# Gate logits taken from channel-major tokens, with mean and deviation applied to the logits

## The chip, the core and the metric

The kernel runs on one core of a Trainium2 chip. The metric is device time in microseconds (us) from the first to the last instruction; before the change its median over 3 runs is 7140.85 us (7115.87 to 7148.11). The engines are TensorE (PE in the profile; PEld is its weight load), VectorE (DVE), ScalarE (ACT), GpSimd (POOL) and SyncE (SP). POOL and SP here mostly issue transfers. Each engine works through its own queue in order; engines wait for one another through semaphores.

## The reference

The input x is 4 x 256 x 64 x 64 in fp32. One MetaFormer layer is computed:

```python
x = x + conv(_ln_c(x))          # three modulated deformable 3x3 convolutions, each with relu
t = tokens(x)                   # 4 x 4096 tokens of 256 channels
t = t + ffn(_ln_t(t))           # mixture of 8 experts, the best 2 of each token
x = from_tokens(t)
```

`_ln_t` normalises a token over its 256 channels: (t - m) / sqrt(v + 1e-5). In the feed-forward part, with z the normalised tokens:

```python
logits = z @ gate_w + gate_b            # 256 x 8
probs = softmax(logits)
top2_vals, top2_idx = top_k(probs, 2)
out = sum over the two experts e of  prob_e * (gelu(z @ W1[e] + b1[e]) @ W2[e] + b2[e])
```

## The kernel before, in words

A batch is cut into 8 blocks of 512 positions (`BLK`), a block into 4 tiles of 128 tokens (`TPB`). The twelve stages (`self.stages`) are pairs of convolution layer and batch; each goes through 8 blocks, and each block through 9 taps. For a tap, GpSimd gathers four corners for 128 positions at a time (L494), VectorE blends them in two steps (L500, L505), ScalarE scales the sample (L508), TensorE transposes it (L523), ScalarE copies it out of PSUM (L526), and TensorE multiplies it with the weights of the tap into `acc` (L546). This is the main line of the program.

All other work is hung beside it in small pieces. Generators are put on a side list by `aside(steps, gen)`, and after every tap `step(k)` takes a share of that list, so that it is empty at the end of the block (`step` divides what is left by the taps that are left). The list is first in, first out. The expert work, the routing and the final sums are in three further lists, taken by `pump` after every tap. A scheduler then orders the instructions of each engine; `self.after(self.last)` asks that an operation is not placed ahead of the newest sample operation.

`tokens` (from L578) is the generator that the change touches. It runs once for each block of the third convolution layer, so in stages 3, 6, 9 and 11 (counted from 0), 32 times in all. Before the change it has 9 pieces:

1. the load of x for the residual,
2. the residual sum, `r` (L590), channel-major: channels on the partitions,
3. eight transposes of `r` into `tok`, token-major (L599), two copies out of PSUM (L604), and the store of `tok`,
4. the first half of `normalise`: mean and variance (L59, L60), square root on ScalarE (L62),
5. the second half: reciprocal (L65) and the normalised tokens `z` (L67); the store of `z` to DRAM, from which the experts later gather,
6. and 7. for two tiles each: four transposes of `z` back to channel-major (L622), a copy to `zT` (L628), the gate products (L632: the stationary operand is `zT`, the moving one the 8 gate columns), a copy of the logits to `lg` (L639),
8. gate bias, maximum, difference, exponential (L646 to L654),
9. softmax, rank of each expert, the two weights (L658 to L679).

`normalise` is also used ahead of the first convolution, by `pre_block`, whose pieces run beside stages 0, 3 and 6. All PSUM tiles tagged `tp` (transposes, logits, and others) share a pool of 3 buffers, `ps`. The tiles `zT` share 2 buffers with the experts' own `zT`. Tiles in the pool `small`, among them the mean and variance `mv`, the reciprocal `rs`, the logits `lg` and the probabilities `pr`, have one buffer each.

An fp32 product stands in the trace as two matmul records, a transpose as one.

Of the kernel before, what the change touches and what calls it, by code (L numbers as in the profile page):

```python
# [8 lines left out]
F32 = mybir.dt.float32  # L9
I32 = mybir.dt.int32  # L10
AF = mybir.ActivationFunctionType
ALU = mybir.AluOpType
AX = mybir.AxisListType

P = 128
H = W = 64
C = 256
CC = C // P
K = 9
NL = 3  # L20
TPB = 4
# [10 lines left out]
E = 8  # L32
# [19 lines left out]

def normalise(nc, pool, src, dst, eps, nm):

    T = src.shape[1]
    mv = pool.tile([P, T, nc.vector.BN_AGGR_DIM], F32, tag="mv", name=f"mv_{nm}")
    for t in range(T):
        st = pool.tile([P, nc.vector.BN_STATS_DIM], F32, tag="st", name=f"st_{nm}_{t}")
        nc.vector.bn_stats(st, src[:, t, :])  # L59
        nc.vector.bn_aggr(mv[:, t, :], st)  # L60
    sd = pool.tile([P, T], F32, tag="sd", name=f"sd_{nm}")
    nc.scalar.activation(sd, mv[:, :, 1], AF.Sqrt, bias=eps)  # L62
    yield
    rs = pool.tile([P, T], F32, tag="rs", name=f"rs_{nm}")
    nc.vector.reciprocal(rs, sd)  # L65
    for t in range(T):
        nc.vector.tensor_scalar(  # L67
            dst[:, t, :], src[:, t, :], mv[:, t, 0:1], rs[:, t : t + 1], ALU.subtract, ALU.mult
        )
# [37 lines left out]
class Weave:  # L107
# [94 lines left out]
    def ffn_constants(self):  # L202
        nc, cst, ins = self.nc, self.cst, self.ins
        self.t_dram = [
            [
                self.dram.tile([P, TPB, C], F32, name=f"t_{b}_{n}", tag=f"t_{b}_{n}")
                for n in range(NB)
            ]
            for b in range(self.B)
        ]  # L210
        nf = max(g.NF for g in self.groups)
        for g in self.groups:
            g.zd = self.dram.tile([g.M * P, C], F32, name=f"z_{g.nm}", tag=f"z_{g.nm}")
        self.ys = [
            self.dram.tile([nf * FT, C], F32, name=f"ys_{i}", tag=f"ys_{i}") for i in range(3)
        ]
        self.gw = cst.tile([P, CC, E], F32, name="gw")
        nc.sync.dma_start(self.gw, ins["gate_w"].rearrange("(c p) e -> p c e", p=P))
        self.gb = cst.tile([P, E], F32, name="gb")
        nc.sync.dma_start(self.gb, ins["gate_b"])  # L220

        self.before = cst.tile([P, E, E], F32, name="before")
        nc.vector.memset(self.before, 0.0)
        for e in range(1, E):
            nc.vector.memset(self.before[:, e, 0:e], 1.0)
        self.ones = cst.tile([P, P], F32, name="ones")
        nc.vector.memset(self.ones, 1.0)

        self.upper = cst.tile([P, P], F32, name="upper")
        nc.gpsimd.affine_select(  # L230
            self.upper, self.ones, pattern=[[1, P]], base=0, channel_multiplier=-1,
            compare_op=ALU.is_gt, fill=0.0,
        )

        self.fresh = {}
        for M in {g.M for g in self.groups}:
            fresh = cst.tile([P, E, M], F32, name=f"fresh_{M}")
            nc.vector.memset(fresh, 1.0)
            nc.vector.memset(fresh[:, :, 0:1], 0.0)
            self.fresh[M] = fresh  # L240
        part_i = cst.tile([P, 1], I32, name="part_i")
        nc.gpsimd.iota(part_i, pattern=[[0, 1]], base=0, channel_multiplier=1)
        self.part = cst.tile([P, 1], F32, name="part")
        nc.vector.tensor_copy(self.part, part_i)

        row_i = self.big.tile([P, P], I32, tag="hv", name="row_i")
        nc.gpsimd.iota(row_i, pattern=[[1, P]], base=0, channel_multiplier=0)
        self.row_f = cst.tile([P, P], F32, name="row_f")
        nc.vector.tensor_copy(self.row_f, row_i)
        assert FU * nf <= P  # L250
        self.token = cst.tile([P, NB * TPB], F32, name="token")
        nc.vector.tensor_scalar(
            self.token, self.row_f[:, : NB * TPB], float(P), self.part, ALU.mult, ALU.add
        )


        self.w = None
# [274 lines left out]
    def finish(self):  # L532

        if self.pend is None:
            return
        nc = self.nc
        i, n, k, sT, wins = self.pend
        self.pend = None
        l, b = self.stages[i]
        nm = f"{i}_{n}"  # L540
        if k == 0:
            self.acc = self.ps1.tile([P, CC, BLK], F32, tag="acc", name=f"acc_{nm}")
        acc = self.acc
        for o in range(CC):
            for c in range(CC):
                nc.tensor.matmul(  # L546
                    acc[:, o, :],
                    lhsT=self.wk[k][:, c, o * P : (o + 1) * P],
                    rhs=sT[:, c, :],
                    start=(k == 0 and c == 0),  # L550
                    stop=(k == K - 1 and c == CC - 1),
                )
        if n == NB - 1 and i + 1 < len(self.stages):
            self.load_tap(self.stages[i + 1][0], k, i + 1)
        if k < K - 1:
            return
        bk = self.bk[l]
        if l < NL - 1:
            w = wins[n] = self.window(n, nm, False)
            dst = [w[:, o, 1 : RPB + 1, :] for o in range(CC)]  # L560
            src = [acc[:, o, :].rearrange("p (r w) -> p r w", w=W) for o in range(CC)]
        else:
            r = self.big.tile([P, CC, BLK], F32, tag="a", name=f"r_{nm}")
            dst = [r[:, o, :] for o in range(CC)]
            src = [acc[:, o, :] for o in range(CC)]

        for o in range(CC):
            nc.scalar.activation(dst[o], src[o], AF.Relu, bias=bk[:, o : o + 1], scale=0.5)
        if l < NL - 1:
            self.rows_done(l + 1, b, n, wins)  # L570
        else:
            self.aside(9, self.tokens(b, n, r))

# [2 lines left out]
    def tokens(self, b, n, r):  # L578

        nc = self.nc  # L580
        nm = f"tok_{b}_{n}"
# [11 lines left out]
        z = self.big.tile([P, TPB, C], F32, tag="b", name=f"z_{nm}")  # L593
        lg = self.small.tile([P, TPB, E], F32, tag="lg", name=f"lg_{nm}")
        for t0 in range(0, TPB, 2):
            tp = self.ps.tile([P, 2, C], F32, tag="tp", name=f"tp_{nm}_{t0}")
            for t in range(2):
                for o in range(CC):
                    nc.tensor.transpose(  # L599
                        tp[:, t, o * P : (o + 1) * P],  # L600
                        r[:, o, (t0 + t) * P : (t0 + t + 1) * P],
                        self.ident,
                    )
            nc.scalar.copy(tok[:, t0 : t0 + 2, :], tp)  # L604
        nc.sync.dma_start(self.t_dram[b][n], tok)
        yield
        rest = normalise(nc, self.small, tok, z, self.eps_t, nm)
        with self.after(self.last):
            next(rest)
        yield  # L610
        with self.after(self.last):
            next(rest, None)
# [1 line left out]
        nc.sync.dma_start(  # L614
            grp.zd[r0 : r0 + BLK, :].rearrange("(t p) c -> p t c", p=P), z
        )
        for t0 in range(0, TPB, 2):
            yield
            tp = self.ps.tile([P, CC, 2 * P], F32, tag="tp", name=f"ztp_{nm}_{t0}")
            for t in range(2):  # L620
                for c in range(CC):
                    nc.tensor.transpose(  # L622
                        tp[:, c, t * P : (t + 1) * P],
                        z[:, t0 + t, c * P : (c + 1) * P],
                        self.ident,
                    )
            zT = self.ffn.tile([P, CC, 2 * P], F32, tag="zT", name=f"zT_{nm}_{t0}")
            nc.scalar.copy(zT, tp)  # L628
            lp = self.ps.tile([P, 2, E], F32, tag="tp", name=f"lp_{nm}_{t0}")
            for t in range(2):  # L630
                for c in range(CC):
                    nc.tensor.matmul(  # L632
                        lp[:, t, :],
                        lhsT=zT[:, c, t * P : (t + 1) * P],
                        rhs=self.gw[:, c, :],
                        start=(c == 0),
                        stop=(c == CC - 1),
                    )
            nc.scalar.copy(lg[:, t0 : t0 + 2, :], lp)  # L639

        def small(tag, shape):
            return self.small.tile(list(shape), F32, tag=tag, name=f"{tag}_{nm}")

        yield
        with self.after(self.last):
            nc.vector.tensor_tensor(  # L646
                lg, lg, self.gb.unsqueeze(1).to_broadcast([P, TPB, E]), ALU.add
            )
        mx = small("mx", (P, TPB))
        nc.vector.tensor_reduce(mx, lg, AX.X, ALU.max)  # L650
        nc.vector.tensor_tensor(
# [8 lines left out]
        pr = small("pr", (P, TPB, E))  # L660
# [446 lines left out]
```

## Time and profile before

| | |
|---|---|
| time, median of 3 | 7140.85 us |
| span of the profiled execution | 8038.3 us |
| gather of samples, L494, POOL | 3456 x 1054 ns |
| blend, L500 and L505, DVE | 3456 x 743 ns and 3456 x 483 ns |
| scaling of a sample, L508, ACT | 3456 x 508 ns |
| transposes of `z`, L622, PE | 256 x 289 ns |
| copies to `zT`, L628, ACT | 64 x 585 ns |
| gate products, L632, PE | 512 records x 268 ns |
| copies of logits, L639, ACT | 64 x 172 ns |
| small operations on logits, L646, DVE | 32 x 189 ns |

A group's row gives its line, engine, operation, tiles and count, then after the bar its busy time in us and the mean in ns, then after the second bar the idle time of the engine just ahead of it in us, with what ended most of that idle time. A row of windows gives a stretch of the span, its length, and each engine's busy time in it. "remote" and "issue" stand for releases that the profile can't put down to one instruction, and for time without a wait that it shows. The profiled execution is longer than the timed ones; its times are used for their proportions.

### The profile page before, as it was taken

Reading aid. Unit: us, or ns where it says so; the run is one execution under the profiler, and the core shown is the slowest. Engines: PE = TensorE matmul, PEld = TensorE weight load, DVE = VectorE, ACT = ScalarE, POOL = GpSimd, SP = SyncE. Lnnn points to the kernel's source line nnn. Section 1 sums busy time; section 2 is a strip of 40 time slices with the busy share of each in tenths; the row PEclk is TensorE's granted clock in tenths of the full one; section 3 lists DMA queues with packets and bytes.
Section 4 is the critical chain, followed back from the end, with each engine's and each line's share of the span. In section 5 each row is a group of like instructions: output and inputs, shape, how many; then the busy total and the mean of one; then the engine's idle time right before and its main releaser. Section 6 shows DMA issues by size and latency. Waiting matters only on the chain. (4 is left out here: it accounts for less than half of the span.)

```text
span 8038.3 us, 90933 instructions
## 1 busy us (share of the span) xinstructions
PE 6721.1 (84%) x27800; PEld 3792.9 (47%) x27800; DVE 4963.7 (62%) x10828; ACT 3620.7 (45%) x7697; POOL 4458.6 (55%) x4237
## 2 busy tenths in 40 slices
PE   7898888887888888888888888888778888987887
PEld 3443434444444444445454444444444455644665
DVE  6776767777786555556667655555656655557521
ACT  4554544545554444445553444444445444444422
POOL 3554666655556555555546655555545666556543
PEclk8999999999999999998998998999889999998988
DMA  7887989988888777787877888777768778778744
GB/s 245 307 305 281 353 331 333 349 320 297 308 299 297 276 275 280 263 283 265 288 284 251 281 291 297 258 272 281 279 235 291 270 267 277 249 245 285 247 133 127
DMA packets 747781, 2224.89 MB, mean 277 GB/s; under 512 B 100696, under 2 KB 200536, under 8 KB 741536
## 3 DMA queue, kind: packets, MB, share of 16 engines
q0 software_dynamic: 550944, 1946.83, 67.9%
q1 hardware_dynamic: 196352, 272.24, 10.0%
q8 instruction: 225, 3.69, 0.2%
q14 instruction: 260, 2.13, 0.1%
HBM read 2160.68 MB, written 197.44 MB: 293 GB/s over the span
## 5 line engine op out<-in xcount | busy, mean ns | idle before, releaser
L494 POOL DMA_INDIRECT g<-tab,idx x3456 | 3642.4, 1054 | 2424.7 <-DVE s L505 1172.9
L546 PE MATMUL acc<-sT,wk 128*128 128x512 f32 x6912 | 3615.1, 636 | 328.1 <-ACT sT L526 176.4
L500 DVE SCALAR_TENSOR_TENSOR g<-g,cf 128x512 f32<-128x512 f32 x3456 | 2559.2, 743 | 634.2 <-DMA g<-tab,idx 569.4
L505 DVE SCALAR_TENSOR_TENSOR s<-g,cf 128x256 f32<-128x256 f32 x3456 | 1658.2, 483 | 1179.0 <-PE tp L523 643.3
L526 ACT COPY sT<-tp 128x512 f32<-128x512 f32 x1728 | 1005.2, 585 | 2289.2 <-PE tp L523 1532.1
L508 ACT ACTIVATE s<-s,cf 128x256 f32<-128x256 f32 x3456 | 1643.4, 508 | 502.1 <-DVE s L505 313.3
L523 PE MATMUL tp<-ident,s 128*128 128x128 f32 x6912 | 1323.3, 290 | 602.2 <-ACT s L508 385.6
L523 PEld LDWEIGHTS tp<-ident,s 128*128 128x128 f32 x6912 | 896.6, 148 | 1924.4 <-issue 978.4
L546 PEld LDWEIGHTS acc<-sT,wk 128*128 128x128 f32 x6912 | 1222.1, 203 | 1140.8 <-issue 825.4
L859 PE MATMUL py<-w,hT 128*128 128x256 f32 x2608 | 657.0, 394 | 99.4 <-ACT hT L853 42.0
L843 PE MATMUL ph<-fzT,w 128*128 128x256 f32 x2608 | 677.6, 397 | 58.3 <-ACT fzT L832 17.2
L859 PEld LDWEIGHTS py<-w,hT 128*128 128x128 f32 x2608 | 486.7, 195 | 221.5 <-issue 80.9
L843 PEld LDWEIGHTS ph<-fzT,w 128*128 128x128 f32 x2608 | 492.6, 198 | 199.9 <-issue 55.5
L853 ACT ACTIVATE hT<-ph,w 128x256 f32<-128x256 f32 x652 | 283.5, 471 | 588.2 <-PE ph L843 252.8
L895 POOL DMA_INDIRECT gy<-ys,slots x256 | 297.1, 1160 | 419.4 <-DVE ta L910 283.9
L793 POOL DMA_INDIRECT w<-in_W,wrow x163 | 170.7, 1047 | 478.1 <-DVE g L500 118.8
L805 POOL DMA_INDIRECT zt<-z,tok x326 | 329.0, 1009 | 160.6 <-issue 90.2
L349 PE MATMUL po<-win,wo 128*32 128x504 f32 (+1 forms) x2304 | 381.0, 611 | 4.2 <-ACT win L284 2.4
L318 ACT COPY hv<-tpv 128x512 f32<-128x512 f32 x384 | 211.7, 592 | 129.9 <-PE tpv L313 73.9
L877 DVE TENSOR_TENSOR y<-py,w 128x512 f32<-128x512 f32 x163 | 111.6, 685 | 242.7 <-PE py L859 215.4
L349 PE MATMUL po<-win_pre,wo 128*32 128x504 f32 (+1 forms) x1152 | 189.2, 611 | 4.5 <-ACT win_pre L284 3.1
L910 DVE SCALAR_TENSOR_TENSOR ta<-gy,cw,ta 128x256 f32<-128x256 f32 x256 | 120.6, 478 | 93.3 <-DMA gy<-ys,slots 51.2
(159 smaller groups left out, 3593.2 us busy)
## 6 DMA issues: line engine op xcount, KB each, us to landing
tab<-hv SPq DMA_DIRECT2D x384, 256.0 KB
g<-tab,idx POOLq DMA_INDIRECT x3456
ys<-y SPq DMA_DIRECT2D x163, 256.0 KB
wk<-in_conv_w SPq DMA_DIRECT2D x99, 256.0 KB
xc_pre<-in_x SPq DMA_DIRECT2D x32, 512.0 KB
xr_tok<-in_x SPq DMA_DIRECT2D x32, 512.0 KB
t<-t_tok SPq DMA_DIRECT2D x32, 512.0 KB
ta<-t SPq DMA_DIRECT2D x64, 256.0 KB
```

The costliest lines, as they stand in the source:

```text
L349: nc.tensor.matmul(po[g * Q : (g + 1) * Q, :].rearrange("q (r w) -> q r w", w=W)[:, :, x0:x1], lhsT=self.wo[l][:, 3 * ky + kx, c, :], rhs= ...
L494: self.gathered = nc.gpsimd.indirect_dma_start(out=g.rearrange("p x s f -> p (x s f)"), out_offset=None, in_=self.table(*self.stages[i]), ...
L500: nc.vector.scalar_tensor_tensor(g[:, :, 0, :], g[:, :, 1, :], cf[:, j, 0:1], g[:, :, 0, :], ALU.mult, ALU.add,)
L505: self.last = nc.vector.scalar_tensor_tensor(s, g[:, 1, 0, :], cf[:, j, 1:2], g[:, 0, 0, :], ALU.mult, ALU.add)
L508: nc.scalar.activation(s, s, AF.Copy, scale=cf[:, j, 2:3])
L523: self.turned = nc.tensor.transpose(tp[:, c, u * P : (u + 1) * P], ss[u][:, c * P : (c + 1) * P], self.ident)
L526: nc.scalar.copy(self.sT[:, :, t0 * P : (t0 + 2) * P], tp)
L546: nc.tensor.matmul(acc[:, o, :], lhsT=self.wk[k][:, c, o * P : (o + 1) * P], rhs=sT[:, c, :], start=(k == 0 and c == 0), stop=(k == K - 1 ...
L805: self.nc.gpsimd.indirect_dma_start(out=zt, out_offset=None, in_=grp.zd, in_offset=bass.IndirectOffsetOnAxis(ap=grp.tok[:, j : j + 1], axi ...
L843: nc.tensor.matmul(ph[:, h, :], lhsT=w1[:, o : o + P], rhs=zT[:, c, :], start=(c == 0), stop=(c == CC - 1),)
L859: nc.tensor.matmul(py[:, u, :], lhsT=hT[h // 2][:, h % 2, u * P : (u + 1) * P], rhs=w2[:, h * C : (h + 1) * C], start=(h == 0), stop=(h == ...
L895: self.nc.gpsimd.indirect_dma_start(out=g, out_offset=None, in_=self.ys[grp.i % 3], in_offset=bass.IndirectOffsetOnAxis(ap=grp.slots[:, i, ...
```

## The change

For a token t with mean m and deviation s, the logits of the normalised token are ((t - m) / s) @ W = (t @ W - m * sum(W)) / s, where sum(W) adds the gate weights over the channels. So the product can be taken from the tokens before they are normalised, and these stand channel-major in `r` already. The transposes of `z` back and their copies are left out, and the logits of a block are taken in one piece instead of two; mean and reciprocal deviation are applied to the 8 logits of each token. The channel sums of the gate weights (`gsum`) are made once, by a product with ones. `normalise` hands out the mean and the reciprocal for this. `tokens` has 7 pieces in place of 9, and the small operations ahead of the maximum are no longer asked to stand behind the newest sample.

```diff
 def normalise(nc, pool, src, dst, eps, nm):
...
     nc.scalar.activation(sd, mv[:, :, 1], AF.Sqrt, bias=eps)
-    yield
     rs = pool.tile([P, T], F32, tag="rs", name=f"rs_{nm}")
+    yield mv[:, :, 0], rs
     nc.vector.reciprocal(rs, sd)
...
+        self.gsum = cst.tile([P, E], F32, name="gsum")
...
+        gp = self.ps.tile([P, E], F32, tag="tp", name="gp")
+        for c in range(CC):
+            nc.tensor.matmul(
+                gp, lhsT=self.ones, rhs=self.gw[:, c, :], start=(c == 0), stop=(c == CC - 1)
+            )
+        nc.vector.tensor_copy(self.gsum, gp)
...
-            self.aside(9, self.tokens(b, n, r))
+            self.aside(7, self.tokens(b, n, r))
...
             nc.scalar.copy(tok[:, t0 : t0 + 2, :], tp)
+
+        lp = self.ps.tile([P, TPB, E], F32, tag="tp", name=f"lp_{nm}")
+        for t in range(TPB):
+            for c in range(CC):
+                nc.tensor.matmul(
+                    lp[:, t, :],
+                    lhsT=r[:, c, t * P : (t + 1) * P],
+                    rhs=self.gw[:, c, :],
+                    start=(c == 0),
+                    stop=(c == CC - 1),
+                )
+        nc.scalar.copy(lg, lp)
         nc.sync.dma_start(self.t_dram[b][n], tok)
         yield
         rest = normalise(nc, self.small, tok, z, self.eps_t, nm)
         with self.after(self.last):
-            next(rest)
+            mean, rs = next(rest)
...
-        for t0 in range(0, TPB, 2):
-            yield
-            tp = self.ps.tile([P, CC, 2 * P], F32, tag="tp", name=f"ztp_{nm}_{t0}")
-            for t in range(2):
-                for c in range(CC):
-                    nc.tensor.transpose(
-                        tp[:, c, t * P : (t + 1) * P],
-                        z[:, t0 + t, c * P : (c + 1) * P],
-                        self.ident,
-                    )
-            zT = self.ffn.tile([P, CC, 2 * P], F32, tag="zT", name=f"zT_{nm}_{t0}")
-            nc.scalar.copy(zT, tp)
-            lp = self.ps.tile([P, 2, E], F32, tag="tp", name=f"lp_{nm}_{t0}")
-            for t in range(2):
-                for c in range(CC):
-                    nc.tensor.matmul(
-                        lp[:, t, :],
-                        lhsT=zT[:, c, t * P : (t + 1) * P],
-                        rhs=self.gw[:, c, :],
-                        start=(c == 0),
-                        stop=(c == CC - 1),
-                    )
-            nc.scalar.copy(lg[:, t0 : t0 + 2, :], lp)
...
-        with self.after(self.last):
-            nc.vector.tensor_tensor(
-                lg, lg, self.gb.unsqueeze(1).to_broadcast([P, TPB, E]), ALU.add
-            )
+        shift = small("pr", (P, TPB, E))
+        every = [P, TPB, E]
+        nc.vector.tensor_tensor(
+            shift,
+            self.gsum.unsqueeze(1).to_broadcast(every),
+            mean.unsqueeze(2).to_broadcast(every),
+            ALU.mult,
+        )
+        nc.vector.tensor_tensor(lg, lg, shift, ALU.subtract)
+        nc.vector.tensor_tensor(lg, lg, rs.unsqueeze(2).to_broadcast(every), ALU.mult)
+        nc.vector.tensor_tensor(lg, lg, self.gb.unsqueeze(1).to_broadcast(every), ALU.add)
```

## The prediction

> **What bounds the kernel now.** I read the shares of the whole span first, then the costliest groups, then stage windows, then the groups of the token stage, then one block in order of time. One thing comes before all: the profiled execution took 8038.3 us and the timed runs 7140.85 us, so times read off the trace are scaled by 7140.85/8038.3 = 0.888 where they are to stand for timed ones.
>
> ```profile
> PE 6721.1 (84%) x27800; PEld 3792.9 (47%) x27800; DVE 4963.7 (62%) x10828; ACT 3620.7 (45%) x7697; POOL 4458.6 (55%) x4237
> ...
> L546 PE MATMUL acc<-sT,wk 128*128 128x512 f32 x6912 | 3615.1, 636 | 328.1 <-ACT sT L526 176.4
> ...
> L523 PE MATMUL tp<-ident,s 128*128 128x128 f32 x6912 | 1323.3, 290 | 602.2 <-ACT s L508 385.6
> ```
>
> TensorE is the engine nearest to full. Its idle time stands before the transposes of the samples (602 us) and before the convolution products (328 us), and ends mostly on ScalarE. So a microsecond of TensorE work counts nearly in full, and so does a wait that holds up ScalarE just ahead of a sample. Next, windows by stage: stages 2 and 8 hold no token work, 3 and 9 do (window, length, PE busy, then PEld, DVE, ACT, POOL).
>
> ```profile
> 1198.00:1675.00 477.00, 413.15 (x1634) 192.52 (x1634) 354.66 (x698) 235.39 (x520) 309.33 (x288) 0.99 0.92 338
> 1675.00:2247.00 572.00, 467.09 (x1981) 245.23 (x1982) 416.65 (x986) 309.67 (x641) 310.18 (x284) 0.92 0.84 304
> 4828.00:5475.00 647.00, 544.09 (x2153) 297.61 (x2151) 374.58 (x731) 265.44 (x592) 357.72 (x346) 0.92 0.80 281
> 5475.00:6131.00 656.00, 524.18 (x1998) 303.48 (x1999) 390.28 (x815) 299.66 (x619) 330.88 (x326) 0.90 0.74 263
> ```
>
> TensorE idles 13% and 16% in stages 2 and 8, 18% and 20% in stages 3 and 9. Over the four stages with tokens (3, 6, 9, 11) it idles 464 of 2665 us (17.4%), over the eight others 733 of 4830 us (15.2%). The token work costs more than its instructions: 2.2% of 2665 us, about 59 us, is excess idle. Now its groups.
>
> ```profile
> L632 PE MATMUL lp_tok<-gw,zT_tok 128*128 128x8 f32 x512 | 72.2, 268 | 36.4 <-ACT zT_tok L628 22.5 <-issue 13.8
> ...
> L622 PE MATMUL ztp_tok<-ident,z_tok 128*128 128x128 f32 x256 | 43.3, 289 | 7.0 <-DVE z_tok L67 5.4 <-DVE rs_tok L65 1.6
> ...
> L628 ACT COPY zT_tok<-ztp_tok 128x512 f32<-128x512 f32 x64 | 37.4, 585 | 76.0 <-PE ztp_tok L622 43.1 <-remote 29.6 <-issue 2.6
> ...
> L639 ACT COPY lg_tok<-lp_tok 128x16 f32<-128x16 f32 x64 | 11.0, 172 | 114.5 <-PE lp_tok L632 54.6 <-remote 41.8 <-PE tp L523 6.8
> ...
> L646 DVE TENSOR_TENSOR lg_tok<-lg_tok,gb 128x32 f32<-128x32 f32 x32 | 6.0, 189 | 67.3 <-ACT lg_tok L639 57.7 <-issue 9.6
> ...
> L65 DVE RECIPROCAL rs_tok<-sd_tok 128x4 f32<-128x4 f32 x32 | 5.6, 176 | 169.0 <-ACT sd_tok L62 154.5 <-issue 14.4
> ```
>
> Three engines wait in this chain (numbers after the second bar): TensorE 36 us for zT, ScalarE 76 us for the transposes and 115 us for the logits, VectorE 67 us for the logits. One block in order of time shows how (start, length):
>
> ```profile
> 1773.35 0.60 PE L622 MATMUL ztp_tok<-ident,z_tok 128*128 128x128 f32 x4
> ...
> 1773.99 0.58 ACT L628 COPY zT_tok<-ztp_tok 128x512 f32<-128x512 f32 x1 [2.32 <-PE ztp_tok L622]
> ...
> 1774.63 1.06 PE L632 MATMUL lp_tok<-gw,zT_tok 128*128 128x8 f32 x8 [0.68 <-ACT zT_tok L628]
> ...
> 1775.54 0.63 PE L622 MATMUL ztp_tok<-ident,z_tok 128*128 128x128 f32 x4
> ...
> 1776.85 1.06 PE L632 MATMUL lp_tok<-gw,zT_tok 128*128 128x8 f32 x8 [0.68 <-issue]
> ```
>
> From 1773.35 to 1777.91, 4.56 us, TensorE serves only this chain and idles twice for 0.68 us, since nothing else stands between transpose and product in its queue.
>
> **What the Trainium skill says.** "Perfetto Trace Analysis", Identifying the Most-Contended Engine: TensorE's busy time is a poor measure of its limit because matmuls are pipelined. The trace agrees: a transpose lasts 289 ns, yet four take 0.60 us. So I count occupied stretches, not mean durations. "VectorE: DVE Perf Modes", the TRN2 errata section: an fp32 tensor_tensor of N elements takes (N+151)/0.96 ns, an estimate of 191 ns for 32 elements; the trace has 189 ns at L646. "ScalarE: Activation LUTs", What ACT_TABLE_LOAD costs: a switch of table set loads for about 1283 ns; the trace shows 1283 ns ahead of L62 and L654. The square root, the exponential and the order between them stay, so these loads stay.
>
> **The change part by part.** There are 32 token blocks (four batches of eight).
>
> Removed on TensorE: 8 transposes a block, 256. By the stretch of four, 64 x 0.60 = 38 us; by the row's busy time 43 us; by the spacing in a run of eight (L599: 1.04 us for eight at 7609.73, so 0.13 us each) 33 us. I take 38.
>
> Kept on TensorE: the 16 product records a block (L632). Their stationary operand is now r, channel-major, in place of zT: same shape, same count, no gain. They move two pieces forward, beside the transposes of r, and wait for nothing but r, which the transposes have waited for already.
>
> Removed waits on TensorE: 36.4 us ahead of L632 and 7.0 us ahead of L622, 43 us. Some of it only moves, because the work queued next (sample transposes) often waits for ScalarE itself. Between 0 and 43; I take half, 22.
>
> ScalarE: 64 copies of 585 ns go (37 us), and 64 logit copies of 172 ns become 32 of about 190 (11 to 6 us): 43 us less. The four places in each block where its queue stops for TensorE become one. It is 45% busy, so the 43 us are worth nothing by themselves; what counts is that scaled samples (L508) no longer queue behind these stops. That can reach TensorE only through its waits for ScalarE; the excess idle of 59 us bounds it, and the 22 above is my share of that.
>
> VectorE: one add becomes four small operations, three more a block, 96 x 0.189 = 18 us. It is 62% busy. In the order of the built program they stand between sample operations, and the logits arrive before the square root does, so the 67 us wait at L646 should go. The reciprocal (L65), which waits 169 us for the square root, stands behind 5 or 6 VectorE instructions after the last statistic in most blocks instead of 3; a pair of sample operations lasts 743 + 483 ns, so about 1.2 us of each wait (up to 38 us over 32 blocks) is filled with work. I price VectorE at nothing net, hidden by its own idle.
>
> Buffers: the PSUM tiles tagged tp of a block fall from six to three, but the three now come together out of a pool of three. The zT buffers are left to the experts. z is now read only by its store.
>
> Pieces: tokens take 7 turns of the side list, not 9, so other side work comes a step or two earlier. The one-off sum of the gate weights (four product records, one copy) costs under 2 us at the start, before the first gather's stage fills, and is priced at nothing. DMA is unchanged.
>
> Sum: 38 + 22 = 60 us of the trace, times 0.888 = 53 us: 7141 - 53 = 7088 us, 0.75% faster.
>
> **The rivals.** (A) Hidden: in the token stages the pace is set by the chain gather, VectorE, ScalarE, and freed TensorE time turns into more waiting at L523. For it: 385.6 us of waits at L523 end on ScalarE's scaling. Against it: TensorE is busy 80% or more in each of these stages. Only the stretch of 4.56 us shrinks in the last block, where nothing is beside it, and a few more like it: about 10 us, 7130.
>
> (B) Slower: the three tp tiles taken together leave none for samples, and ScalarE's logit copy stands in its queue while TensorE, in the built order, does two or so convolution products (four records at 0.43 us spacing, 1.7 us) and the logit products (1.06 us) first. That is a new wait of at most 2.8 us a block, with sample scaling and the next transposes queued behind it: 32 x 2.8 = 90 us, less 38, is 52, times 0.888 is 46: 7187. Against it: four such ScalarE stops (191 us together at L628 and L639) leave in exchange for this one.
>
> (C) More: all the excess idle of the token stages leaves with the chain: 38 + 59 = 97, times 0.888 = 86: 7055. Against it: the table loads, the waits for square root and exponential (169 and 115 us on VectorE), also token work, remain.
>
> **How the numbers follow.** Forecast 0.47, A 0.25, B 0.14, C 0.14. The range must reach to A and C and to most of B's milder forms; its low end takes C with the 38 us of filled reciprocal waits in part on top (7055 - 25 = 7030), its high end stops short of B at 7175. 0.5% is 36 us: faster is below 7105. Nearly all of the forecast and all of C lie there, 0.59; A and the mild edge of B lie within, 0.27; the rest of B is slower, 0.14.
>
> **What would show it.** Right: no ztp and no zT records; the L632 successor with under 5 us of TensorE idle ahead of it; total TensorE busy down by 33 to 43 us; VectorE's wait for logits under 10 us; the wait at the reciprocal down; idle of TensorE in the token stages nearer 16%. If TensorE's busy time falls and L523's idle rises by as much, A holds. If the logit copy on ScalarE shows a wait of 2 us or more a block, and the copies of samples start later, B holds. What would make the forecast wrong is mainly that the whole interleaving is replanned: gathers, expert steps and table stores all shift by a step in the token stages, and their chance alignments can be worth as much as the 53 us.

## The result, and the profile after

Median of the changed kernel 7061.8 us (7049.3 to 7076.12, four runs), of the kernel before beside it 7138.75 us (four runs): ratio 0.9898, interval 0.9867 to 0.9928. The change makes the kernel 77 us, 1.0%, faster. The forecast was 7088 us.

The profile that the prediction read shows an execution of 8038.3 us, while the kernel before takes 7136 to 7139 us beside all runs below but three, beside which it takes 8050.87 us; these are called the faster and the slower conditions here. So the kernel before was profiled again under the faster conditions (label a0_before, 7130.68 us, ratio 0.9995, interval 0.9987 to 1.0004), and this profile is the one compared from here on. First its page, span and busy times:

```profile
span 7125.6 us, 90933 instructions
...
PE 6448.4 (90%) x27800; PEld 3683.0 (52%) x27800; DVE 4975.3 (70%) x10828; ACT 3626.6 (51%) x7697; POOL 4425.1 (62%) x4237
```

The same two lines of the changed kernel:

```profile
span 7074.4 us, 90366 instructions
...
PE 6415.2 (91%) x27548; PEld 3652.5 (52%) x27548; DVE 4980.0 (70%) x10925; ACT 3595.7 (51%) x7600; POOL 4405.2 (62%) x4237
```

TensorE is 33 us less busy with 252 records less (256 transposes gone, 4 products for the channel sums new), ScalarE 31 us less busy, VectorE 5 us more. By these lines the forecast looks right step by step. The groups say less. Those of before, under the same conditions:

```profile
L523 PE MATMUL tp<-ident,s 128*128 128x128 f32 x6912 | 1282.8, 284 | 314.1 <-ACT s L508 305.9 <-ACT sT L526 4.1 <-ACT lg_tok L639 0.4
...
L632 PE MATMUL lp_tok<-gw,zT_tok 128*128 128x8 f32 x512 | 67.2, 257 | 8.3 <-ACT zT_tok L628 8.3
...
L646 DVE TENSOR_TENSOR lg_tok<-lg_tok,gb 128x32 f32<-128x32 f32 x32 | 6.0, 187 | 19.9 <-ACT lg_tok L639 19.9
...
L658 DVE TENSOR_REDUCE sm_tok<-lg_tok 128x4 f32<-128x32 f32 x32 | 5.9, 184 | 66.7 <-ACT lg_tok L654 66.7
...
L65 DVE RECIPROCAL rs_tok<-sd_tok 128x4 f32<-128x4 f32 x32 | 5.6, 174 | 66.9 <-ACT sd_tok L62 66.9
```

And their counterparts after (lines shift by 9 around the samples; L618 and L625 are the new place of the gate products and of the copy of their logits):

```profile
L532 PE MATMUL tp<-ident,s 128*128 128x128 f32 x6912 | 1285.8, 283 | 298.8 <-ACT s L517 287.2 <-ACT sT L535 5.2 <-ACT hv L327 0.8
...
L618 PE MATMUL lp_tok<-gw,r 128*128 128x8 f32 x512 | 60.8, 254 | 0.0
...
L652 DVE TENSOR_TENSOR lg_tok<-lg_tok,pr_tok 128x32 f32<-128x32 f32 x32 | 6.0, 188 | 0.8
...
L625 ACT COPY lg_tok<-lp_tok 128x32 f32<-128x32 f32 x32 | 6.0, 186 | 38.7 <-PE lp_tok L618 38.7
...
L664 DVE TENSOR_REDUCE sm_tok<-lg_tok 128x4 f32<-128x32 f32 x32 | 5.8, 180 | 9.2 <-ACT lg_tok L660 9.2
...
L66 DVE RECIPROCAL rs_tok<-sd_tok 128x4 f32<-128x4 f32 x32 | 5.6, 175 | 99.6 <-ACT sd_tok L63 99.6
```

The wait of the gate products is gone, but under these conditions it was 8.3 us and not 36.4. The wait for the logits on VectorE is gone (19.9 to 0.8), the wait for the exponential fell from 66.7 to 9.2, and the wait for the square root rose from 66.9 to 99.6. One block in order of time (start, length, then the idle time in brackets) shows the chain that is left:

```profile
1642.30 1.04 PE L608 MATMUL tp_tok<-ident,r 128*128 128x128 f32 x8
...
1643.17 1.92 PE L618 MATMUL lp_tok<-gw,r 128*128 128x8 f32 x16
...
1645.13 0.19 ACT L625 COPY lg_tok<-lp_tok 128x32 f32<-128x32 f32 x1 [0.26 <-PE lp_tok L618]
```

None of this adds up to 77 us, so the next view is by stage. A stage ends with the second eviction of `acc` (the copy of the sums out of PSUM by ScalarE) of its eighth block, and stage 0 is counted from the first sample gather, some 111 us after the start of the span. Two profiled executions of the changed kernel differ by up to 5 us in a stage, so single differences of that size say nothing. Lengths in us:

| stage | 0 | 1 | 2 | 3 | 4 | 5 | 6 | 7 | 8 | 9 | 10 | 11 | rest |
|---|---|---|---|---|---|---|---|---|---|---|---|---|---|
| a0_before | 513 | 488 | 453 | 463 | 509 | 526 | 530 | 641 | 529 | 533 | 698 | 717 | 415 |
| changed kernel (a1_after) | 509 | 488 | 453 | 461 | 513 | 524 | 526 | 647 | 525 | 524 | 664 | 705 | 418 |
| a2_transposes | 517 | 489 | 453 | 458 | 509 | 523 | 528 | 642 | 528 | 519 | 663 | 704 | 420 |
| a3_copies | 509 | 489 | 453 | 458 | 508 | 524 | 528 | 643 | 526 | 516 | 667 | 703 | 422 |
| b1_nine | 512 | 489 | 453 | 469 | 514 | 526 | 525 | 649 | 525 | 519 | 701 | 709 | 416 |
| d1_late | 514 | 489 | 453 | 461 | 507 | 524 | 525 | 639 | 529 | 519 | 699 | 708 | 422 |
| c1_before7 | 517 | 489 | 453 | 468 | 512 | 526 | 534 | 650 | 528 | 523 | 667 | 709 | 415 |
| b3_split | 513 | 489 | 453 | 464 | 513 | 524 | 528 | 645 | 527 | 532 | 701 | 716 | 416 |
| f1_apart_before | 520 | 488 | 453 | 463 | 514 | 524 | 529 | 605 | 525 | 533 | 640 | 688 | 414 |

Stage 10 holds the token work of one block only, the last of stage 9, in its first 70 us or so; yet 34 of the 58 us between the first two rows are there, and only 4 of the 34 fall in that first block. The token stages 3, 6, 9 and 11 give 2, 3, 8 and 13 us. Windows of before, stages 3, 9 and 10 (stretch, length, busy time of PE, PEld, DVE, ACT, POOL, clock, share of the DMA engines, GB/s):

```profile
1566.00:2029.00 463.00, 435.88 (x1981) 235.18 (x1981) 419.02 (x990) 309.70 (x640) 308.50 (x287) 0.99 1.00 382
...
4763.00:5295.00 532.00, 489.42 (x1999) 288.98 (x2000) 390.28 (x815) 298.80 (x618) 327.88 (x327) 0.97 0.90 327
...
5295.00:5994.00 699.00, 609.17 (x2571) 370.09 (x2569) 430.86 (x931) 307.61 (x644) 434.13 (x412) 0.96 0.81 276
```

The same stages after:

```profile
1566.00:2027.00 461.00, 429.33 (x1924) 225.52 (x1924) 418.49 (x1010) 303.94 (x619) 304.75 (x286) 1.00 1.00 384
...
4755.00:5280.00 525.00, 481.67 (x1949) 283.76 (x1949) 398.25 (x843) 287.60 (x597) 336.58 (x331) 0.98 0.92 334
...
5280.00:5949.00 669.00, 604.88 (x2568) 368.50 (x2569) 427.13 (x928) 304.94 (x641) 419.25 (x409) 0.96 0.83 287
```

(These windows are of the first profile of the changed kernel, span 7074.4; the table's row is of a1_after, span 7067.4.) In stage 3 TensorE is 7 us less busy and the stage is 2 us shorter: its share of idle time rises from 5.9 to 6.9%. The share of the DMA engines there is 1.00 before and after, which suggests that the transfers, and not TensorE, set the length of that stage. In stage 10 TensorE has 2571 and 2568 records, and 30 us are gone.

### The profile page after: what moved, and what is told of

Read it like the earlier page. It is cut to its first block, busy times and chain, and to the rows that moved or that the text cites. A ratio compares the mean times of both kernels' runs of the same rounds, so it can differ in the third digit from the quotient of the medians.

```text
span 7074.4 us, 90366 instructions
## 1 busy us (share of the span) xinstructions
PE 6415.2 (91%) x27548; PEld 3652.5 (52%) x27548; DVE 4980.0 (70%) x10925; ACT 3595.7 (51%) x7600; POOL 4405.2 (62%) x4237
## 5 line engine op out<-in xcount | busy, mean ns | idle before, releaser
L503 POOL DMA_INDIRECT g<-tab,idx x3456 | 3590.6, 1039 | 1662.7 <-issue 725.1
L555 PE MATMUL acc<-sT,wk 128*128 128x512 f32 x6912 | 3462.3, 612 | 148.8 <-ACT sT L535 138.0
L532 PEld LDWEIGHTS tp<-ident,s 128*128 128x128 f32 x6912 | 877.7, 144 | 1582.9 <-ACT s L517 855.1
L555 PEld LDWEIGHTS acc<-sT,wk 128*128 128x128 f32 x6912 | 1167.6, 194 | 893.9 <-issue 596.8
L532 PE MATMUL tp<-ident,s 128*128 128x128 f32 x6912 | 1285.8, 283 | 298.8 <-ACT s L517 287.2
L849 PE MATMUL ph<-fzT,w 128*128 128x256 f32 x2608 | 656.2, 388 | 36.6 <-DMA w<-in_W,wrow 20.7
L865 PE MATMUL py<-w,hT 128*128 128x256 f32 x2608 | 642.8, 389 | 35.3 <-ACT hT L859 28.3
```

What stands on the lines that cost most here:

```text
L503: self.gathered = nc.gpsimd.indirect_dma_start(out=g.rearrange("p x s f -> p (x s f)"), out_offset=None, in_=self.table(*self.stages[i]), ...
L532: self.turned = nc.tensor.transpose(tp[:, c, u * P : (u + 1) * P], ss[u][:, c * P : (c + 1) * P], self.ident)
L555: nc.tensor.matmul(acc[:, o, :], lhsT=self.wk[k][:, c, o * P : (o + 1) * P], rhs=sT[:, c, :], start=(k == 0 and c == 0), stop=(k == K - 1 ...
L849: nc.tensor.matmul(ph[:, h, :], lhsT=w1[:, o : o + P], rhs=zT[:, c, :], start=(c == 0), stop=(c == CC - 1),)
L865: nc.tensor.matmul(py[:, u, :], lhsT=hT[h // 2][:, h % 2, u * P : (u + 1) * P], rhs=w2[:, h * C : (h + 1) * C], start=(h == 0), stop=(h == ...
```

## The experiments

All ratios are to the kernel before run beside it, with the 95% interval. The kernel before took 7135.76 us beside the runs whose labels begin with a, and 7137.09 beside b1, b3, c1 and d1. Two of them set the frame:

> The kernel before, unchanged, profiled once more, since its first profiled execution was 12.6% longer than its timed ones. Every theory expects a ratio of 1.000 within 0.3% and a span near 7140 us. It gives the profile against which the changed one can be compared engine by engine. If TensorE's busy time here is 33 to 43 us above the 6415 us of the changed kernel, the removed work is as large as forecast; if the idle ahead of the transposes and products of samples is larger here by 20 us or more, waits made up the rest.

> The changed kernel again, as the mark for the runs beside it. Expected 0.990 of the kernel before, about 7062 us, by every theory.

a1_after, the changed kernel again: 7063.12 us, 0.9887 (0.9872 to 0.9902). The gain holds on another occasion.

**Is it the removed work? Put it back.** Two kernels add the removed work to the changed kernel, with results that nobody reads.

```diff
 # a2_transposes: changed kernel, piece 6 of tokens
+        for t0 in range(0, TPB, 2):
+            tp = self.ps.tile([P, CC, 2 * P], F32, tag="tp", name=f"ztp_{nm}_{t0}")
+            for t in range(2):
+                for c in range(CC):
+                    nc.tensor.transpose(tp[:, c, t * P : (t + 1) * P],
+                        z[:, t0 + t, c * P : (c + 1) * P], self.ident)
 # a3_copies: the same, and in the loop over t0
+            zT = self.ffn.tile([P, CC, 2 * P], F32, tag="zT", name=f"zT_{nm}_{t0}")
+            nc.scalar.copy(zT, tp)
```

> The changed kernel with the eight transposes of z put back in each block, into PSUM tiles that nobody reads; no copies, no products from them. Theory of work (TensorE time counts in full): 38 us slower than the changed kernel (33 to 43), so about 7100 us, 0.995 of before. Theory of waits (the chain transpose, copy, product, copy was the cost): under 12 us slower, about 7070 us. Theory of a new plan of the interleaving: no fixed sign, anything within 20 us of the changed kernel.

> As the run before it, and ScalarE copies the transposed z into zT as well; the gate products still read r, so nothing but the buffers waits for the copies. This puts back all removed work of TensorE and most of ScalarE's (64 copies of 585 ns, 37 us) but not the chain. Theory of work on TensorE: like the run with transposes alone, about 7100 us. If ScalarE's queue is what counts (copies ahead of the scaling of samples): 20 us or more above the run with transposes alone. Theory of waits: still nearer the changed kernel than the one before, under 7100 us.

a2_transposes: 7064.55 us, 0.9887 (0.9871 to 0.9903). a3_copies: 7053.43 us, 0.9876 (0.9861 to 0.9891). The work is there in the groups of a3_copies:

```profile
L647 PE MATMUL ztp_tok<-ident,z_tok 128*128 128x128 f32 x256 | 38.4, 281 | 1.7 <-DVE z_tok L68 1.7
...
L653 ACT COPY zT_tok<-ztp_tok 128x512 f32<-128x512 f32 x64 | 36.2, 587 | 41.9 <-PE ztp_tok L647 41.8
```

38 us of TensorE and 36 us of ScalarE, with 42 us of new waiting on ScalarE, cost nothing that can be measured: the two intervals of a1_after and a2_transposes leave room for about 17 us by estimate, not for 38. What these kernels don't put back is the order transpose, copy, product: their products still come from `r`.

Where the samples are short shows in the groups of a0_before, followed back from TensorE's wait at L523:

```profile
L508 ACT ACTIVATE s<-s,cf 128x256 f32<-128x256 f32 x3456 | 1653.0, 509 | 683.8 <-DVE s L505 669.8
...
L505 DVE SCALAR_TENSOR_TENSOR s<-g,cf 128x256 f32<-128x256 f32 x3456 | 1659.2, 483 | 671.2 <-PE tp L523 396.4
...
L500 DVE SCALAR_TENSOR_TENSOR g<-g,cf 128x512 f32<-128x512 f32 x3456 | 2562.5, 744 | 684.7 <-DMA g<-tab,idx 679.9
```

TensorE waits for ScalarE, ScalarE for VectorE, and VectorE 680 us for gathers to land; another 396 us VectorE waits for TensorE to read a sample. By these rows TensorE sets the pace for part of the time only, and late gathers for another part.

**Is it TensorE's wait in the chain?** b3_split is the kernel before with the chain cut: all eight transposes and their copies in one piece, all products and one copy of logits in the next, still nine pieces in all.

```diff
 # b3_split: kernel before
+        yield
+        zT = self.big.tile([P, CC, BLK], F32, tag="a", name=f"zT_{nm}")
         for t0 in range(0, TPB, 2):
-            yield
...
+            nc.scalar.copy(zT[:, :, t0 * P : (t0 + 2) * P], tp)
+        yield
+        lp = self.ps.tile([P, TPB, E], F32, tag="tp", name=f"lp_{nm}")
+        for t in range(TPB):
...
+        nc.scalar.copy(lg, lp)
```

> The kernel before with nine pieces and all its work, but the chain pulled apart: all eight transposes of z and their copies in one piece, all gate products and one copy of logits in the next, with zT for the whole block in another buffer. It takes away the waits of the chain and leaves work and plan. Theory of the plan: no change beyond 0.3%, 7115 to 7150 us. Theory of waits: half or more of the gain, 7060 to 7100 us.

b3_split: 7131.66 us, 0.9993 (0.9985 to 1.0001). The wait of TensorE for `zT` falls from 8.3 to 0.3 us, and that is worth nothing measurable. The waits of the other two engines mostly stay: ScalarE's for the products goes from 64.1 to 51.4 us, VectorE's for the exponential from 66.7 to 68.1. So this run doesn't show what those are worth.

**Is it the number of pieces?** b1_nine gives the changed kernel its nine pieces back (two empty ones); c1_before7 gives the kernel before seven, with all its work.

```diff
 # b1_nine: changed kernel
-            self.aside(7, self.tokens(b, n, r))
+            self.aside(9, self.tokens(b, n, r))
...
         yield
+        yield
+        yield
         shift = small("pr", (P, TPB, E))
 # c1_before7: kernel before
-            self.aside(9, self.tokens(b, n, r))
+            self.aside(7, self.tokens(b, n, r))
...
         for t0 in range(0, TPB, 2):
-            yield
+            if t0 == 0:
+                yield
...
-        yield
         with self.after(self.last):
```

> The changed kernel with nine pieces again: two empty pieces after the store of z, so that its small operations, and the start of the routing after the last block of a batch, fall on the taps they had before. Its work is that of the changed kernel. New leading theory, of the plan: putting back transposes and copies cost nothing, and 34 of the 58 us that the two profiles differ by lie in stage 10, which holds no token work but the expert steps and final sums whose start the token pieces set; so the gain comes from pieces of the later lanes falling one tap earlier. It expects most of the gain lost: 7105 to 7130 us, 0.995 to 0.999, with stage 10 back near 695 us. Rival, of waits (the chain transpose, copy, product, copy itself cost the time, also in stages 9 and 11): 7060 to 7075 us, 0.989 to 0.991.

> The kernel before with its whole gate chain (both halves: transposes, copies, products, then bias to exponential) in one piece, so seven in all; all its work and its waits stay, and the chain is even closer packed. Theory of the plan: most of the gain without any of the saved work, 7060 to 7095 us, 0.989 to 0.994, stage 10 near 665 us. Theory of waits: no gain or a loss, 7130 to 7170 us, 0.999 to 1.005.

b1_nine: 7121.9 us, 0.9981 (0.9974 to 0.9989), 15 us faster than before. c1_before7: 7102.47 us, 0.9954 (0.9941 to 0.9966), 35 us faster without one operation removed. So the pieces alone, with all the work and the chain kept, bring more than the saved work and the cut chain bring in nine pieces. In the table, stage 10 goes with the pieces: 663 to 667 us in a1, a2, a3 and c1, which have seven, 698 to 701 in a0, b1 and b3, which have nine.

**Which effect of the pieces?** The last piece of a group's last block calls `enqueue`, which starts the routing. With nine pieces it falls on the ninth tap, with seven on the eighth. d1_late keeps seven pieces in all blocks but the last of each group, where two empty pieces stand just ahead of `enqueue`.

```diff
 # d1_late: changed kernel
-            self.aside(7, self.tokens(b, n, r))
+            late = any(g.b == b and g.n1 - 1 == n for g in self.groups)
+            self.aside(9 if late else 7, self.tokens(b, n, r))
...
         if n == grp.n1 - 1:
+            yield
+            yield
             self.enqueue(grp)
```

> The changed kernel with seven working pieces everywhere, but the last block of each group of batches has two empty ones just ahead of the routing, so that only the start of routing, experts and sums moves back to the tap it had before. Theory of the plan, with the start of the lanes as its cause: most of the gain of stage 10 lost, 7095 to 7125 us, 0.994 to 0.998. If the plan matters by the places of the token pieces themselves: 7060 to 7070 us, as the changed kernel. Theory of waits: the same 7060 to 7070 us.

d1_late: 7105.16 us, 0.9962 (0.9947 to 0.9976), and stage 10 is back at 699 us. A start of routing one tap later gives back 41 us: a1_after gains 73 us on the kernel before beside it, d1_late 32. The other 32 us don't come from that start.

**What a tap changes in stage 10.** Two lanes run there beside the samples, each at one unit per two taps: the final sums of one batch (`combine_fetch`, two gathers into `gy`, then `combine`, two additions into `ta`) and the experts of the next (weights `w`, tokens `zt`). All their gathers share GpSimd's queue with the sample gathers. One tap after the other, "." a sample gather, y a sum's gather, w weights, z tokens, the order read off the traces is

```
before, b1_nine, d1_late:   ...yy.zz   ..w..     ...yy.zz   ..w..
changed kernel, c1_before7: ..wyy..    ....zz    ..wyy..    ....zz
f1_apart_before (below):    ....zzyy   ..w..     ....zzyy   ..w..
```

What GpSimd waits for in stage 10 of before (us in total, times, longest):

```profile
POOL gy L895 <- DVE ta L910: 97.8, 33, 5.4
...
POOL w L793 <- ACT s L508: 11.4, 9, 2.9
```

The same for the changed kernel (a1_after):

```profile
POOL w L799 <- ACT s L517: 37.9, 11, 6.1
POOL gy L901 <- DVE ta L916: 34.5, 10, 5.1
```

d1_late, stage 10:

```profile
POOL gy L904 <- DVE ta L919: 98.8, 37, 5.5
```

c1_before7, stage 10:

```profile
POOL w L793 <- ACT s L508: 41.4, 13, 5.3
POOL gy L895 <- DVE ta L910: 35.4, 11, 5.5
```

In these rows `gy` and `w` together stand 109 us in before and 72 us after: 37 us less, where the stage is 34 us shorter. Over the whole span the same two rows stand 320 and 273 us: 47 us less, beside 73 us of time. One such stand in before, first on GpSimd, then on VectorE, in order of time:

```profile
5636.60 1.03 POOL L494 DMA_INDIRECT g<-tab,idx  x1 [0.30 <-issue]
5643.03 1.43 POOL L895 DMA_INDIRECT gy<-ys,slots  x1 [5.40 <-DVE ta L910]
5644.77 0.95 POOL L895 DMA_INDIRECT gy<-ys,slots  x1 [0.30 <-DVE s L505]
5646.03 0.95 POOL L494 DMA_INDIRECT g<-tab,idx  x1 [0.30 <-issue]
...
5641.00 0.75 DVE L500 SCALAR_TENSOR_TENSOR g<-g,cf 128x512 f32<-128x512 f32 x1 [3.56 <-DMA g<-tab,idx]
...
5642.29 0.48 DVE L910 SCALAR_TENSOR_TENSOR ta<-gy,cw,ta 128x256 f32<-128x256 f32 x1
```

`gy` has four buffers, two sums' worth, and the program queues the gathers of sum m+2 right after sum m, in the same tap. They can't start until the addition (L910) has freed a buffer. That addition stands in VectorE's queue behind a sample operation (L500), which waits 3.56 us for its own gather to land. GpSimd meanwhile stands 5.40 us at the head of its queue, and the next sample gathers stand behind it. So VectorE soon lacks samples again: the two engines hand each other the delay.

**Take that stand away.** f1_apart_before is the kernel before with one edit: a sum's gathers come one tap after the sum that frees their buffers; two taps a sum, as before.

```diff
 # f1_apart_before: kernel before, end()
             if m + 1 < grp.M:
-                put(0, lambda m=m: self.combine_fetch(grp, m + 1))
-            put(2, lambda m=m: self.combine(grp, m))
+                put(1, lambda m=m: self.combine_fetch(grp, m + 1))
+            put(1, lambda m=m: self.combine(grp, m))
```

> Once more the kernel before with the fetches for the sums one tap after the sum that frees their buffers; its first run fell on a chip on which the kernel before takes 8051 us. On a chip where that takes about 7137 us: if GpSimd's standing at these fetches (about 98 us in stage 10, against 35 in the changed kernel) is what costs stage 10 its 35 us, that wait falls below 50 us, stage 10 falls from 698 to 660 to 675 us, and the time to 7095 to 7115 us, 0.994 to 0.997. If the crowding of the tap (two sum fetches and two token fetches between the gathers) is what costs, the wait falls but stage 10 stays above 690 us and the time at 7125 to 7145 us. On the slower chip again: 1.008 to 1.013, with stage 10 near 774 us.

f1_apart_before: 7003.15 us (6992.73 to 7006.16) against 7138.23 for the kernel before: 0.9807 (0.9793 to 0.9820). It is 135 us faster than before and the fastest kernel of these runs, without one arithmetic operation removed, in nine pieces, with all transposes of `z`. Its waits in stage 10:

```profile
POOL gy L895 <- DVE ta L910: 31.7, 13, 5.1
...
POOL w L793 <- ACT s L508: 7.5, 6, 2.1
```

Its timeline there, where the sum's gathers follow the tokens' without a stand:

```profile
5568.58 1.48 POOL L805 DMA_INDIRECT zt<-z,tok  x1 [0.30 <-issue]
5570.37 1.15 POOL L895 DMA_INDIRECT gy<-ys,slots  x1 [0.30 <-DVE s L505]
5571.82 0.97 POOL L895 DMA_INDIRECT gy<-ys,slots  x1 [0.30 <-issue]
5573.10 0.97 POOL L494 DMA_INDIRECT g<-tab,idx  x1 [0.30 <-issue]
```

Stage 10 is 640 us against 698, and stages 7 and 11, where sums run too, are 37 and 29 us shorter (table). Over the whole span the wait of `gy` for `ta` falls from 261 to 123 us, 138 us for 135 us of time. The rival of a crowded tap falls: `zzyy` still stand in one tap, and the time is gone. So the stand of GpSimd at the sums' gathers costs time nearly in full under these conditions: that is shown. And the page of this kernel has a lesson on the view from which the forecast began:

```profile
span 7004.5 us, 90988 instructions
...
PE 6403.8 (91%) x27800; PEld 3663.6 (52%) x27800; DVE 4975.6 (71%) x10828; ACT 3623.3 (52%) x7697; POOL 4460.4 (64%) x4237
```

TensorE is 45 us less busy than in a0_before with the same 27800 records. The granted clock accounts for that: it was 0.977 on average here and 0.970 in a0_before, and busy time times clock is 6257 and 6255 us. In the slower first profile, 6721.1 us at 0.930, it is 6251. So TensorE's busy time also changes without any change of its work. In stages 7, 10 and 11 the clock went from 0.94, 0.96 and 0.93 to 0.97, 0.97 and 0.96; why is not shown. By the same measure, and by estimate since the clock has three digits, the changed kernel's TensorE work is about 26 us smaller (6415.2 us at 0.971 make 6229), not 33, and in a2_transposes about 22 us of it are back (6411.0 at 0.975 make 6251) at no cost in time that can be measured.

**Three runs under the slower conditions** (kernel before: 8050.87 us). They were to separate the order of the queue from the earlier start, and to try the split of sums.

```diff
 # e1_route1: kernel before; one group's routing a tap later, which turns the order as in the changed kernel
-        put(0, lambda: self.route(grp))
+        put(1 if grp.i == 2 else 0, lambda: self.route(grp))
 # e3_apart_after: the edit of f1_apart_before in the changed kernel
 # e4_apart_before: the kernel f1_apart_before
```

> The kernel before with all its work, its nine pieces and its chain, but the routing of the third batch starts one tap later still. In GpSimd's queue this turns the two rhythms of stage 10, both two taps long, against each other: the fetches for the final sums of one batch then stand in the tap of the experts' weight fetch, as in the changed kernel, and no longer in the tap of the experts' token fetches. Theory of the rhythm: stage 10 falls from 698 us to 660 to 672 us and the time to 7095 to 7110 us, 0.994 to 0.997. Theory that an earlier start is what helps: no gain or a small loss, 7130 to 7145 us. Theory of waits or work in the gate chain: no change, 7130 to 7140 us.

> The changed kernel with the fetches for the sums issued one tap after the sum that frees their buffers, not in the same tap: the lane's cost of two taps is split in one for the fetch and one for the sum. If GpSimd standing at a sum's fetch, with the gathers of samples queued behind it, is what costs time in stage 10, the wait of those fetches for VectorE (197 us over the span) falls below 100 us and stage 10 below 660 us; 7020 to 7050 us, 0.984 to 0.988. If the rhythm acts in another way (transfers that collide): no change or a loss, 7060 to 7085 us.

> The same split in the kernel before, where the fetches for the sums then still stand in the tap of the token fetches. If the standing of GpSimd is the whole cause: stage 10 falls to about 660 us, as in the changed kernel, and the time to 7090 to 7105 us, 0.993 to 0.996. If the company in the tap is the cause (six transfers between the gathers of one tap): stage 10 stays above 690 us and the time at 7125 to 7140 us.

e1_route1: 8118.66 us, 1.0081 (1.0056 to 1.0106). e3_apart_after: 8096.42, 1.0053 (1.0037 to 1.0068). e4_apart_before: 8145.95, 1.011 (1.0084 to 1.0137). All three are slower, and e4 is the very kernel that gains 1.9% under the faster conditions. Here stage 10 grows from 708 to 772 us in e1_route1, whose queue has the order `..wyy..` of the changed kernel; its waits there:

```profile
POOL w L793 <- ACT s L508: 137.7, 16, 18.0
...
POOL gy L895 <- DVE ta L910: 41.9, 10, 7.9
```

The stand at `gy` falls there too (from 91.4 us in the first profile of before to 41.9), but the weights' gather, some 9 us at a time, takes its place. Stage 10 of e4_apart_before has 89 us of the weights' wait and is 774 us long, though its stand at `gy` is down to 37.5 us. The changed kernel itself was not run under these conditions, nor e1 and e3 under the faster ones. The expectations speak of a faster and a slower chip; the record has the same chip number for these three runs and for f1_apart_before, so whether the chip or something else makes the difference is open.

## Why the prediction was right, and where it was wrong

The direction was right, and the size within the range: 77 us where 53 were forecast. The cause named for it was mostly wrong, so it is luck that the number fell within the range: the two terms that made up the 53 us are not what brought the gain, and a term priced at nothing brought 35 to 41 of 73 us.

- **"A microsecond of TensorE work counts nearly in full": wrong.** This is the step that failed first, and with it the 38 us of the sum. Putting 256 transposes back costs 0.0% (0.9887 both times). TensorE at 90% busy does not set the pace throughout: the prediction followed its waits back to ScalarE and stopped there, while the wait behind that runs on to VectorE and to gathers that have not landed (680 us at L500; in the prediction's own profile 569 us). Even stage 6, where TensorE is busy 524.7 of 529 us, is only 3 us shorter in the changed kernel, although seven blocks' transposes are gone from it, some 7 us by estimate at 0.13 us each. The section of the Trainium skill that the prediction drew on ("Perfetto Trace Analysis", Identifying the Most-Contended Engine) says that busy time is a poor measure of how near TensorE is to its limit. The prediction used that to price one transpose and did not apply it to the 84%.
- **The waits, 22 us: wrong.** Taking TensorE's wait out of the kernel before gives 0.9993 (0.9985 to 1.0001). The size was off as well: the 36.4 us ahead of L632, of which that view puts 22.5 down to `zT`, and the 67 us ahead of L646 belonged to the slower conditions; they are 8.3 and 19.9 us under those of the timed runs. The factor 0.888 scaled all times alike, and waits do not scale so. The excess idle of 59 us, which was to bound this term, is not there either: in a0_before TensorE idles 7.3% of the four token stages and 9.3% of the eight others.
- **"Pieces: tokens take 7 turns of the side list, not 9": priced at nothing, and the largest term.** c1_before7 has this part alone and gains 35 us; d1_late takes the earlier start of routing back and loses 41 of 73 us. What goes with it is a stand of GpSimd: the wait at the sums' gathers in stage 10 falls from 98 to 35 us. The prediction named a replanned interleaving only as what could make it wrong.
- **VectorE at nothing net: not contradicted, one direction wrong.** Four small operations in place of one are there (5 us more busy in all), and the wait for the logits is gone as said. The wait for the square root was to fall and rose, 66.9 to 99.6 us; it is the exponential's wait that fell, 66.7 to 9.2.
- **ScalarE "worth nothing by itself": right.** a3_copies puts 36 us of copies back at no cost.
- **Rival A (work hidden): its mechanism held** as far as the put-back work goes, though not its time of 7130. But the rise at L523 that was to show it did not come: that idle time fell from 314.1 to 298.8 us. **Rival B:** the wait at the new logit copy is there, 38.7 us over 32 blocks, 1.2 us each instead of up to 2.8, and no stage shows a loss that follows it. **Rival C** came nearest in time, 7055, but the share of idle time in the token stages 3 and 9 did not fall (5.9 to 6.9%, 8.0 to 8.3%).

What stays open: saved work under the old plan (b1_nine) is worth 15 us, yet neither the work put back nor the cut of b3_split shows it, so it can't be given to one of them. The gains of 8 and 13 us in stages 9 and 11 are not explained; a2 and a3 have them with the work put back, and c1_before7 has 10 and 8 with the chain in place as well. In stage 9 one wait goes along with them: VectorE waits 33 to 40 us there for the exponential in a0, b3 and f1, whose stage takes 532 to 533 us, and 0 to 5.4 us in the other six kernels of the table, whose stage takes 516 to 524. No run changes that wait alone, and in stage 11 it is 0 in all nine. For stage 10, both an earlier start and the turned order of the queue come with the changed kernel; f1_apart_before shows that the stand itself costs, but the two were not tried apart under the faster conditions. And whether the change gains under the slower ones is not known.

## What to carry to other kernels

An engine that is 90% busy need not be the limit: look for an in-order queue whose head stands at something issued in the same step, with the bound engine's input queued behind it, even if that queue's engine is busy only 62% of the time. An edit that takes pieces out of a cooperative schedule also shifts everything that starts after them; compare stage by stage, and start with the stages that the edit hardly touches. To learn what removed work was worth, put it back alone. And a profile taken under other conditions than the timed runs misleads on waits above all: 36.4 us there were 8.3 here.

## What the runs showed of the hardware

- The same kernel takes 7136 to 7139 us beside some runs and 8050.87 us beside others, with a mean granted TensorE clock of 0.97 and 0.93, and an edit worth 1.9% beside the first loses 1.1% beside the others.
- Issuing one gather of samples holds GpSimd 1.05 us on average over 3456 (0.95 us and more in the lines shown), mostly with 0.30 us to the next; a gather whose buffer was not free stood 5.40 us, and the sample gathers issued after it came only then.
- TensorE's busy time differed by 45 us between two kernels with the same number of records; times the granted clock, the two agree to 2 us.
- Eight fp32 gate products of 8 columns, sixteen records, take 1.92 us, 0.12 us a record, hardly less than 0.13 us for a transpose of 128 columns (eight in 1.04 us).
